# Two convolution products begun on three quarters of their columns, four tiles normalized inside attention, the last tile stored in halves

## The chip, the cores and the metric

The kernel runs on one core of a Trainium2 chip. A core has TensorE (PE, matrix products into PSUM), VectorE (DVE), ScalarE (ACT) and GpSimd (POOL), each with its own in-order queue of instructions, and SyncE (SP), whose queue here only issues DMAs; ACT's and POOL's queues issue DMAs as well. The metric is device microseconds of one execution, the median over several runs. The trace comes from one further, profiled execution.

## The reference

One sequence of T = 2048 rows of D = 1024 in float32 goes through three residual steps:

```
x = x + 0.5 * ffn(layernorm(x))
x = x + attn(layernorm(x))
x = x + 0.5 * ffn(layernorm(x))      # the same weights as the first

ffn(x):  routing = softmax(x @ gate_w.T)                 # 8 experts
         out = ((x * (routing @ in_scale)) @ sign(weight).T) * (routing @ out_scale) + bias
attn(x): q, k, v = split(conv1d(x, conv_w, width 3) + conv_b)   # 3 x 256 channels
         q, k, v -> 16 heads of 64 (wq, wk, wv and biases)
         causal softmax attention in blocks of 128 rows
         out = (heads @ wo + bo) @ proj_w + proj_b
```

## The kernel before

**Tiles and stages.** A tile is 128 rows; there are NT = 16. The first FFN goes through the tiles and, two tiles behind, normalizes its own results (`norm_x2`) and transposes them into windows for the convolution (`transpose_x2`). Then come the convolution, attention in 4 groups of 4 tiles with 8 head pairs each (32 steps), and the second FFN, which is the same class `Ffn` on other rows.

**The convolution** has width 3 and is computed with 8 transformed products per 6 rows of output, in place of 18. The transformed inputs are V[0] to V[7], each of NQ = 342 columns for each of the 8 chunks of channels; the transformed weights are the taps themselves for k = 0 and 7 (`gs`, loaded by `load_g`) and sums of them for k = 1 to 6 (`us`, made by `taps_begin` and `taps_end`). Three tiles make a window; windows 0 to 4 give 64 columns each and window 5, which has tile 15 alone, gives 22. V[0] and V[7] of a window are made by `end_transform` (three DVE instructions) as soon as the window is whole: windows 0 to 3 have their V[0] long before tile 15 is done, window 4 after tile 14, window 5 after tile 15. `store_window` makes V[7] and writes the window to DRAM; `load_window` reads it back (tile `xl`) for V[1] to V[4] (`transform`, in `conv_ends`) and once more for V[5] and V[6] (`last_transforms`), which take the memory of V[0] and V[7]. `transform` writes column a with L462, L463 and L467, column b with L466, and reads the window with L462 to L465.

**Products.** `product` takes a PSUM bank, runs 8 matmuls over the chunks (the trace shows 16 instructions, two for each float32 matmul) and has ACT copy the result out. `conv_ends` runs all six channel blocks (WORDER) with k = 0, then all six with k = 7; after that every block does k = 1 to 6 in pairs. The end of a k = 0 product frees the slot (six in `cwp`) into which SP loads the block's third tap.

**Order.** The framework places each engine's instructions at build: it simulates the program with its own estimates and takes, at each step, the earliest traced instruction that is ready. `pin` (`keep_in_program_order`) puts an instruction behind the one that was traced just ahead of it on its engine. At run time each engine goes through its fixed order.

**The second FFN's start.** `fill` returns the parts of the second FFN that run while attention drains; from step i = 32 on, one part is taken after the second and one after the fourth stage of a step. `stage_proj` of the last group is called at i = 36, ahead of the part of that place. `run` then goes through the tiles: gate of t + 2, scale of t + 1, the first half of `main`, the transposes of t + 3, the statistics of t + 4 (`norm`), the second half. `normalize` is two `bn_stats` (L155) and three small operations on DVE and POOL, and one ACT pass into `xn`. `add_bias` adds the bias to the row by a DMA on POOL's queue. A row takes one of 8 slots (`rring`): `load_rows2` fetches it, `store` writes it out.

Of the kernel before, what the change touches and what calls it, by code (L numbers as in the profile page):

```python
# [24 lines left out]
def kernel(  # L25
# [146 lines left out]
    class Ffn:  # L172
# [3 lines left out]

        def __init__(self, name, sw, work, xnp, first, end, row, ahead, after, between, beside):
            self.name, self.sw, self.work, self.xnp, self.first, self.end = name, sw, work, xnp, first, end  # L180
            self.row, self.ahead, self.after, self.between, self.beside = row, ahead, after, between, beside
            self.xns, self.xnTs, self.lgps, self.routs, self.rTs, self.oscs, self.ys = ({} for _ in range(7))
# [95 lines left out]
        def main(self, t, *halves, between=None, at=DC - 2):  # L278
            y, osc, xrow = self.ys[t], self.oscs[t], self.row(t)
            pms = {h: bank("mm", [P, NB], f"pm_{self.name}_{t}_{h}") for h in halves}  # L280
            for c in range(DC):
                if between and c == at:
                    between()
                for h, pm in pms.items():
                    for n in range(2):
                        nc.tensor.matmul(  # L286
                            pm,
                            lhsT=y[:, n, c, :],
                            rhs=self.sw[:, c, ts(h, NB)],
                            start=(c == 0 and n == 0),  # L290
                            stop=(c == DC - 1 and n == 1),
                        )
            for h, pm in pms.items():
                o, xt = osc[:, ts(h, NB)], xrow[:, ts(h, NB)]
                nc.vector.tensor_tensor(pm, pm, o, ALU.mult)  # L295
                nc.vector.tensor_tensor(xt, xt, pm, ALU.add)  # L296
            if NH2 - 1 in pms:
                del self.ys[t], self.oscs[t]

        def fill(self):  # L300

            a = self.first
            return [
                lambda: (self.norm(a), self.add_bias(a), self.norm(a + 1, True), self.add_bias(a + 1)),
                lambda: self.on(self.transpose, a),
                lambda: self.on(self.gate, a),
                lambda: (self.on(self.route, a), self.on(self.transpose, a + 1)),
                lambda: (self.on(self.turn, a), self.on(self.gate, a + 1)),
                lambda: self.scale(a, out=True),
                lambda: (self.on(self.route, a + 1), self.norm(a + 2, True), self.add_bias(a + 2)),  # L310
                lambda: (self.on(self.transpose, a + 2), self.on(self.turn, a + 1)),
                lambda: (self.norm(a + 3, True), self.add_bias(a + 3)),
            ]

        def on(self, stage, t, *more):
# [3 lines left out]
        def run(self):  # L319

            for t in range(self.first, self.end):
                self.on(self.gate, t + 2)
                if t + 1 in self.ys:
                    self.out_scale(t + 1)
                elif t + 1 < self.end:
                    self.scale(t + 1, out=True)
                route, turn = (lambda stage=stage: self.on(stage, t + 2) for stage in (self.route, self.turn))
                begun = t not in self.ys  # L330
                if begun:
                    route()
                else:
                    self.main(t, 0, between=route, at=DC // 2)
                self.on(self.transpose, t + 3)
                self.on(self.between, t - 2)
                self.on(self.norm, t + 4, t == self.first)
                self.on(self.add_bias, t + 4)
                if begun:
                    turn()  # L340
                else:
                    self.main(t, 1, between=turn, at=DC // 2)
                self.on(self.after, t - 1)
                self.beside(t)
# [50 lines left out]
    def transpose_x2(t):  # L395
        xn = x2ns.pop(t)
        n, third = divmod(t, 3)
        xw = window(n)
        at = third * P

        head = -at % 6
        tail = (at + P) % 6
        for h in range(DC // 4):
            tr = bank("acc", [P, 4, P], f"tr2_{t}_{h}")
            for c in range(4):
                nc.tensor.transpose(tr[:, c, :], xn[:, ts(4 * h + c, P)], ident)
            rows6 = xw[:, 4 * h : 4 * h + 4, :].rearrange("p c (k q) -> p c k q", q=ROW)
            q, whole = (at + head) // 6, (P - head - tail) // 6
            copy = nc.vector.tensor_copy if (t, h) == (NT - 1, 1) else nc.scalar.copy
            copy(  # L410
                rows6[:, :, :, ds(q, whole)],
                tr[:, :, head : P - tail].rearrange("p c (q k) -> p c k q", k=6),
            )
            if head:
                copy(rows6[:, :, 6 - head : 6, q - 1], tr[:, :, 0:head])
            if tail:
                copy(rows6[:, :, 0:tail, q + whole], tr[:, :, P - tail : P])
        if third == 2 or t + 1 == NT:
            end_transform(n, 0)
        if third == 0 and n > 0:  # L420
            nc.gpsimd.tensor_copy(xws[n - 1][:, :, RIGHT : RIGHT + 1], xw[:, :, 0:1])
            if t + 1 < NT:
                store_window(n - 1)
        if t == NT - 3:
            window(TRIPLES - 1)
        if third == 2 and n + 1 < TRIPLES:
            nc.gpsimd.tensor_copy(window(n + 1)[:, :, LEFT : LEFT + 1], xw[:, :, LEFT + QT : LEFT + ROW])
# [3 lines left out]
    def columns(k, n):  # L431
        return V[k][:, :, ds(n * QT, SIZES[n])]

    def end_transform(n, k):
        d = tokens(xws[n], n)
        a, b, c, e = (d[0], d[2], d[4], d[6]) if k == 0 else (d[7], d[5], d[3], d[1])
        v = columns(k, n)
        nc.vector.tensor_tensor(v, c, b, ALU.subtract)
        nc.vector.scalar_tensor_tensor(v, v, 5.25, a, ALU.mult, ALU.add)
        nc.vector.tensor_tensor(v, v, e, ALU.subtract)  # L440

    def store_window(n):
        end_transform(n, NK - 1)
        nc.sync.dma_start(out=win_dram[n], in_=xws[n])

    def load_window(n, pl):
# [61 lines left out]

    turns = iter(range(NW * NK))

    def product(w, k, uk, mp):

        acc = bank(("mm", "acc")[next(turns) // 2 % 2], [P, NQ], f"cv_{w}_{k}")
        for c in range(DC):
            nc.tensor.matmul(acc, lhsT=uk[:, c, :], rhs=V[k][:, c, :], start=(c == 0), stop=(c == DC - 1))  # L515
        m = ms.setdefault(w, {})
        m[k] = mp.tile([P, NQ], F32, name=f"m_{w}_{k}", tag=f"m{k}", bufs=NW if k in (0, NK - 1) else 1)
        if k == 1:
            nc.scalar.activation(m[k], acc, AF.Identity, bias=conv_b_sb[:, w : w + 1], scale=SCALES[k])
        else:  # L520
            nc.scalar.mul(m[k], acc, SCALES[k])  # L521

    def conv_ends(mp, tf, up, xs):
# [7 lines left out]
        for at in range(2 * NW):  # L531
            last, i = divmod(at, NW)
            w = WORDER[i]
            product(w, last * (NK - 1), gs[w, 2 * last], mp)
            if at == 0:
                for n in (TRIPLES - 2, TRIPLES - 1):
                    store_window(n)
            if not last:
                load_g(w, 2)
                if w == begun:  # L540
                    taps_begin(w, PAIRS[0], up)
                    taps_begin(w, PAIRS[1], up)
            elif i == 0:
                load_g(w, 1)
            elif i < 4:
                load_g(WORDER[1], (1, 2, 0)[i - 1])
            n, *more = jobs[at // 2]
            transform(n, 1 + 2 * (at % 2), tf)
            if more and at % 2:
                load_window(*more)  # L550
# [124 lines left out]
        ffn.run()  # L675
    norm_x2(NT - 1)
    transpose_x2(NT - 2)
    transpose_x2(NT - 1)
    ring.close()
    up = pool(b1, "up", 1)  # L680
    vm = pool(b1, "vm", 1)
# [60 lines left out]

    def store(t):
        nc.sync.dma_start(out=out[ts(t, P), :], in_=rows.pop(t))

    with ExitStack() as ph:
        ow = pool(ph, "ow", 1)
# [175 lines left out]
        for i in range(len(steps) + len(stages)):  # L923
            for n, stage in enumerate(stages):
                if 0 <= i - n < len(steps):
                    stage(*steps[i - n])
                if n == 0 and i == len(steps) - 1:

                    b2.close()
                    work = pool(f2, "work2", 2, side="right")  # L930
                    ffn = Ffn("f2", sw2, work, work, 0, NT, lambda t: rows[t], load_rows2, store, lambda t: None, lambda t: None)
                    parts = ffn.fill()
                if n == 1 and ended is not None:
                    stage_proj(ended)
# [6 lines left out]
    for part in parts:  # L941
        part()
    ffn.run()
    store(NT - 1)
    f2.close()
    b3.close()

# [52 lines left out]
```

## Time and profile before

| what | value |
|---|---|
| three runs | 995.36, 997.54, 998.24 us; median 997.54 |
| profiled execution | 995.0 us, of which the trace's span is 992.9 |
| granted TensorE clock, mean | 0.987 of full |
| FFN main product L286, 1024 matmuls | 266.6 us of PE |
| convolution L515, 768 matmuls | 223.2 us of PE |
| DMA | 143.08 MB, mean 144 GB/s |
| stretch 188 to 207 us | PE busy 11.18 of 19.00 us, clock 0.90 |
| stretch 826 to 853 us | PE busy 22.40 of 27.00 us, clock 0.94 |
| stretch 853 to 973 us | PE busy 119.52 of 120.00 us, clock 1.00 |

Times in the trace count from its first instruction. "L286" is line 286 of the kernel before. An engine's wait is put down to the instruction that released it last.

### The profile page before, as it was taken

To read this page: it belongs to the slowest core of one execution; us is meant where nothing else is said; L and a number is where in the kernel's file an instruction comes from. 1 tells how busy PE (TensorE), PEld (TensorE's weight loads), DVE (VectorE), ACT (ScalarE), POOL (GpSimd) and SP (SyncE) were. 2 spreads that over 40 slices of the span, in tenths; PEclk is the share of its full clock that TensorE was granted. 3 is DMA by queue.
4 is the path that set the end of the run, shared out by engine and by line. 5 is a ranking of instruction groups with operands and counts; after the bars stand their busy time and mean duration, and the time that the engine had idled before them with its cause. 6 is when DMAs were issued, how large, how long until landed. Compare 5 with 4: busy or idle time off the path is not lost.

```text
span 992.9 us, 13803 instructions
## 1 busy us (share of the span) xinstructions
PE 957.5 (96%) x5036; PEld 622.8 (63%) x5036; DVE 653.7 (66%) x1231; ACT 407.7 (41%) x1113; POOL 256.4 (26%) x327
## 2 busy tenths in 40 slices
PE   5999999979999999999999999999999999899997
PEld 4778888746666666655555455545554556677776
DVE  5878887798795665637656465546555656777664
ACT  4476765401011111125546244536442653545440
POOL 4455543310011111003313120212022312534321
PEclk8999999989999999999999999999999999999999
DMA  9766554698787764326030430053004217655421
GB/s 271 208 180 195 157 171 153 229 362 300 279 257 178 202 174 123 96 101 228 18 111 1 168 109 1 0 196 102 1 1 170 44 36 209 161 162 158 110 79 64
DMA packets 37252, 143.08 MB, mean 144 GB/s; under 512 B 4345, under 2 KB 5369, under 8 KB 34754
## 3 DMA queue, kind: packets, MB, share of 16 engines
q1 hardware_dynamic: 27616, 101.35, 28.0%
q0 software_dynamic: 8544, 29.64, 15.7%
q10 hardware_dynamic: 1026, 11.22, 2.9%
q8 instruction: 40, 0.66, 0.3%
q14 instruction: 26, 0.21, 0.1%
HBM read 84.37 MB, written 41.04 MB: 126 GB/s over the span
## 4 chain that ended last, share of the span: by engine, by line
PE 47%; issue 26%; DVE 11%; DMA 7%; POOL 6%; ACT 1%; SPq 0%; POOLq 0%; DVEq 0%; ACTq 0%
PE pm_f L286 18%; PE cv L515 16%; POOL xr L774 3%; PE tr_f L199 2%; PE pp L908 2%; DMA xl<-win 2%; POOL p L830 2%; PE acc L889 1%; PE lgp_f L207 1%; PE is_f L250 1%; DVE st_f L155 1%; DMA g<-in_conv_w_dram 1%; PE pq L797 1%; DMA pw_sb<-in_proj_w_dram 1%; DMA xf<-x 1%
## 5 line engine op out<-in xcount | busy, mean ns | idle before, releaser
L286 PE MATMUL pm_f<-sw,y_f 128*128 128x512 f32 x1024 | 266.6, 408 | 0.2 <-DVE x L296 0.2
L286 PEld LDWEIGHTS pm_f<-sw,y_f 128*128 128x128 f32 x1024 | 186.8, 191 | 40.9 <-DVE x L296 0.4
L515 PE MATMUL cv<-v,u 128*128 128x342 f32 x576 | 166.3, 450 | 1.1 <-DVE u L506 1.1
L515 PEld LDWEIGHTS cv<-v,u 128*128 128x128 f32 x576 | 109.0, 189 | 58.2 <-ACT m L521 1.6
L830 POOL TENSOR_SCALAR_AFFINE_SELECT p<-p 128x512 f32<-128x512 f32 x64 | 40.0, 654 | 285.9 <-ACT p L828 285.9
L843 ACT ACTIVATE p<-p,anm 128x128 f32<-128x128 f32 x256 | 99.0, 388 | 17.5 <-DVE anm L840 17.5
L264 POOL TENSOR_TENSOR y_f<-xnT_f,y_f 128x512 fp32r<-128x512 f32 x64 | 81.3, 1288 | 70.0 <-ACT y_f L263 69.2
L521 ACT ACTIVATE m<-cv 128x342 f32<-128x342 f32 x42 | 19.0, 456 | 165.8 <-PE cv L515 148.6
L828 ACT COPY p<-sc 128x512 f32<-128x512 f32 x64 | 34.3, 587 | 111.2 <-PE sc L818 111.1
L840 DVE TENSOR_REDUCE anm<-p 128x4 f32<-128x512 f32 x64 | 40.9, 681 | 49.9 <-POOL p L830 49.9
L889 PE MATMUL acc<-oT,wo_sb 128*128 128x512 f32 x128 | 66.9, 615 | 0.5 <-DVE oT L881 0.5
L515 PE MATMUL cv<-v,g 128*128 128x342 f32 x192 | 56.9, 459 | 4.7 <-DVE v L440 4.7
L295 DVE TENSOR_TENSOR pm_f<-pm_f,os_f 128x512 f32<-128x512 f32 x64 | 44.3, 692 | 25.8 <-PE pm_f L286 25.6
L797 PE MATMUL pq<-qkv,wq_sb 128*128 128x512 f32 x128 | 61.0, 596 | 0.0
L797 PE MATMUL pq<-qkv,wk_sb 128*128 128x512 f32 x128 | 60.1, 592 | 0.0
L908 PE MATMUL pp<-pw_sb,o2T 128*128 128x512 f32 x128 | 57.6, 600 | 0.5 <-DVE xr L916 0.3
L781 PE MATMUL pv<-wv_sb,qkv 128*128 128x512 f32 x128 | 56.1, 592 | 0.0
L515 PEld LDWEIGHTS cv<-v,g 128*128 128x128 f32 x192 | 37.0, 194 | 24.3 <-DVE v L440 4.9
L506 DVE SCALAR_TENSOR_TENSOR u<-g,u 128x1024 f32<-128x1024 f32 x18 | 22.0, 1223 | 40.3 <-issue 30.7
L200 ACT COPY xnT_f<-tr_f 128x512 f32<-128x512 f32 x60 | 32.5, 589 | 37.7 <-PE tr_f L199 37.7
L843 ACT ACTIVATION_READ_ACCUMULATOR p<-p,anm 128x1 f32 x256 | 47.9, 187 | 0.0
L851 DVE TENSOR_TENSOR p<-p,asum 128x512 f32<-128x512 f32 x64 | 45.6, 712 | 2.2
(143 smaller groups left out, 1482.4 us busy)
## 6 DMA issues: line engine op xcount, KB each, us to landing
g<-in_conv_w_dram SPq DMA_DIRECT2D x28, 512.0 KB, 5.3
u<-in_conv_w_dram POOLq DMA_DIRECT2D x24, 512.0 KB, 6.3
xl<-win ACTq DMA_DIRECT2D x7, 1560.0 KB, 10.9
win<-xw SPq DMA_DIRECT2D x6, 1560.0 KB, 6.0
x<-in_x_dram SPq DMA_DIRECT2D x16, 512.0 KB, 4.6
raw<-in_weight_t_dram SPq DMA_DIRECT2D x16, 512.0 KB, 6.9
x<-hbias POOLq DMA_DIRECT2D x16, 512.0 KB, 5.8
x<-x SPq DMA_DIRECT2D x16, 512.0 KB, 5.2
```

The lines of the kernel that those rows point to most:

```text
L264: nc.gpsimd.tensor_tensor(yl, y, yh.bitcast(F32), ALU.subtract)
L286: nc.tensor.matmul(pm, lhsT=y[:, n, c, :], rhs=self.sw[:, c, ts(h, NB)], start=(c == 0 and n == 0), stop=(c == DC - 1 and n == 1),)
L295: nc.vector.tensor_tensor(pm, pm, o, ALU.mult)
L515: nc.tensor.matmul(acc, lhsT=uk[:, c, :], rhs=V[k][:, c, :], start=(c == 0), stop=(c == DC - 1))
L781: nc.tensor.matmul(pv, lhsT=qkvs[g][2][:, c, ts(b, P)], rhs=wv_sb[:, c, ts(half, NB)], start=(c == 0), stop=(c == WC - 1),)
L797: nc.tensor.matmul(pq, lhsT=w_sb[:, c, ts(hp, P)], rhs=qkvs[g][n][:, c, :], start=(c == 0), stop=(c == WC - 1),)
L830: nc.gpsimd.affine_select(out=p, in_=p, pattern=[[0, BPG], [-1, P]], compare_op=ALU.is_ge, fill=NEG_INF, base=0, channel_multiplier=1,)
L840: nc.vector.tensor_reduce(nmax, p, AX.X, ALU.max, negate=True)
L843: nc.scalar.activation(p[:, b, :], p[:, b, :], AF.Exp, bias=nmax[:, b : b + 1], accum_out=asum[:, b : b + 1],)
L851: nc.vector.tensor_tensor(p, p, asum.unsqueeze(2).broadcast_to([P, BPG, P]), ALU.mult)
L889: nc.tensor.matmul(accs[g][m], lhsT=wo_sb[:, hp, ts(m, P)], rhs=oT, start=(hp == 0), stop=(hp == NHP - 1),)
L908: nc.tensor.matmul(pp, lhsT=o2T[:, m, ts(b, P)], rhs=pw_sb[:, m, ts(h, NB)], start=(m == 0), stop=(m == WC - 1),)
```

## The change

It has three parts.

1. `product_columns` computes a product on a range of columns. After `transpose_x2(NT - 2)` the first block's k = 0 product runs on its first 256 columns (FIRST = 4 x 64, windows 0 to 3), after `transpose_x2(NT - 1)` the second block's. `product` later does the remaining 86 columns of these two, and all columns of the others. Tile 15's second half is copied into its window by ACT in place of DVE. `store_window` of windows 4 and 5 pins its DVE instructions.
2. `fill` normalizes tiles 0, 1 and 2 in its first part and tile 3 in its eighth, ahead of the last group's `stage_proj` (before: tiles 0 and 1 in the first, tile 2 in the seventh, tile 3 in the ninth, behind that `stage_proj`). The second FFN takes `xn` from a pool of its own with three buffers (before: two, in `work2`), and its statistics in `run` are pinned for every tile (before: for tile 4 alone).
3. `leave` stores the last tile's halves, each behind its half of `main`; `store(NT - 1)` at the end goes away.

```diff
--- before.py
+++ after.py
@@ -176,7 +176,8 @@
 
 
 
-        def __init__(self, name, sw, work, xnp, first, end, row, ahead, after, between, beside):
+        def __init__(self, name, sw, work, xnp, first, end, row, ahead, after, between, beside, kept=1, leave=None):
+            self.kept, self.leave = kept, leave or (lambda t, h: None)
             self.name, self.sw, self.work, self.xnp, self.first, self.end = name, sw, work, xnp, first, end
             self.row, self.ahead, self.after, self.between, self.beside = row, ahead, after, between, beside
             self.xns, self.xnTs, self.lgps, self.routs, self.rTs, self.oscs, self.ys = ({} for _ in range(7))
@@ -294,6 +295,7 @@
                 o, xt = osc[:, ts(h, NB)], xrow[:, ts(h, NB)]
                 nc.vector.tensor_tensor(pm, pm, o, ALU.mult)
                 nc.vector.tensor_tensor(xt, xt, pm, ALU.add)
+                self.leave(t, h)
             if NH2 - 1 in pms:
                 del self.ys[t], self.oscs[t]
 
@@ -301,15 +303,14 @@
 
             a = self.first
             return [
-                lambda: (self.norm(a), self.add_bias(a), self.norm(a + 1, True), self.add_bias(a + 1)),
+                lambda: [(self.norm(t, t > a), self.add_bias(t)) for t in range(a, a + 3)],
                 lambda: self.on(self.transpose, a),
                 lambda: self.on(self.gate, a),
                 lambda: (self.on(self.route, a), self.on(self.transpose, a + 1)),
                 lambda: (self.on(self.turn, a), self.on(self.gate, a + 1)),
                 lambda: self.scale(a, out=True),
-                lambda: (self.on(self.route, a + 1), self.norm(a + 2, True), self.add_bias(a + 2)),
-                lambda: (self.on(self.transpose, a + 2), self.on(self.turn, a + 1)),
-                lambda: (self.norm(a + 3, True), self.add_bias(a + 3)),
+                lambda: (self.on(self.route, a + 1), self.on(self.transpose, a + 2)),
+                lambda: (self.on(self.turn, a + 1), self.norm(a + 3, True), self.add_bias(a + 3)),
             ]
 
         def on(self, stage, t, *more):
@@ -334,7 +335,7 @@
                     self.main(t, 0, between=route, at=DC // 2)
                 self.on(self.transpose, t + 3)
                 self.on(self.between, t - 2)
-                self.on(self.norm, t + 4, t == self.first)
+                self.on(self.norm, t + 4, t < self.kept)
                 self.on(self.add_bias, t + 4)
                 if begun:
                     turn()
@@ -406,7 +407,7 @@
                 nc.tensor.transpose(tr[:, c, :], xn[:, ts(4 * h + c, P)], ident)
             rows6 = xw[:, 4 * h : 4 * h + 4, :].rearrange("p c (k q) -> p c k q", q=ROW)
             q, whole = (at + head) // 6, (P - head - tail) // 6
-            copy = nc.vector.tensor_copy if (t, h) == (NT - 1, 1) else nc.scalar.copy
+            copy = nc.scalar.copy
             copy(
                 rows6[:, :, :, ds(q, whole)],
                 tr[:, :, head : P - tail].rearrange("p c (q k) -> p c k q", k=6),
@@ -431,16 +432,17 @@
     def columns(k, n):
         return V[k][:, :, ds(n * QT, SIZES[n])]
 
-    def end_transform(n, k):
+    def end_transform(n, k, pinned=False):
         d = tokens(xws[n], n)
         a, b, c, e = (d[0], d[2], d[4], d[6]) if k == 0 else (d[7], d[5], d[3], d[1])
         v = columns(k, n)
-        nc.vector.tensor_tensor(v, c, b, ALU.subtract)
-        nc.vector.scalar_tensor_tensor(v, v, 5.25, a, ALU.mult, ALU.add)
-        nc.vector.tensor_tensor(v, v, e, ALU.subtract)
-
-    def store_window(n):
-        end_transform(n, NK - 1)
+        kept = pin if pinned else lambda ins: None
+        kept(nc.vector.tensor_tensor(v, c, b, ALU.subtract))
+        kept(nc.vector.scalar_tensor_tensor(v, v, 5.25, a, ALU.mult, ALU.add))
+        kept(nc.vector.tensor_tensor(v, v, e, ALU.subtract))
+
+    def store_window(n, pinned=False):
+        end_transform(n, NK - 1, pinned)
         nc.sync.dma_start(out=win_dram[n], in_=xws[n])
 
     def load_window(n, pl):
@@ -508,11 +510,25 @@
 
     turns = iter(range(NW * NK))
 
+    accs = {}
+    FIRST = 4 * QT
+
+    def product_columns(w, k, uk, lo, hi):
+        if (w, k) not in accs:
+            accs[w, k] = bank(("mm", "acc")[next(turns) // 2 % 2], [P, NQ], f"cv_{w}_{k}")
+        for c in range(DC):
+            nc.tensor.matmul(
+                accs[w, k][:, lo:hi],
+                lhsT=uk[:, c, :],
+                rhs=V[k][:, c, lo:hi],
+                start=(c == 0),
+                stop=(c == DC - 1),
+            )
+
     def product(w, k, uk, mp):
 
-        acc = bank(("mm", "acc")[next(turns) // 2 % 2], [P, NQ], f"cv_{w}_{k}")
-        for c in range(DC):
-            nc.tensor.matmul(acc, lhsT=uk[:, c, :], rhs=V[k][:, c, :], start=(c == 0), stop=(c == DC - 1))
+        product_columns(w, k, uk, FIRST if (w, k) in accs else 0, NQ)
+        acc = accs.pop((w, k))
         m = ms.setdefault(w, {})
         m[k] = mp.tile([P, NQ], F32, name=f"m_{w}_{k}", tag=f"m{k}", bufs=NW if k in (0, NK - 1) else 1)
         if k == 1:
@@ -534,7 +550,7 @@
             product(w, last * (NK - 1), gs[w, 2 * last], mp)
             if at == 0:
                 for n in (TRIPLES - 2, TRIPLES - 1):
-                    store_window(n)
+                    store_window(n, True)
             if not last:
                 load_g(w, 2)
                 if w == begun:
@@ -675,7 +691,10 @@
         ffn.run()
     norm_x2(NT - 1)
     transpose_x2(NT - 2)
+
+    product_columns(WORDER[0], 0, gs[WORDER[0], 0], 0, FIRST)
     transpose_x2(NT - 1)
+    product_columns(WORDER[1], 0, gs[WORDER[1], 0], 0, FIRST)
     ring.close()
     up = pool(b1, "up", 1)
     vm = pool(b1, "vm", 1)
@@ -742,6 +761,11 @@
 
     def store(t):
         nc.sync.dma_start(out=out[ts(t, P), :], in_=rows.pop(t))
+
+    def leave(t, h):
+
+        if t + 1 == NT:
+            nc.sync.dma_start(out=out[ts(t, P), ts(h, NB)], in_=rows[t][:, ts(h, NB)])
 
     with ExitStack() as ph:
         ow = pool(ph, "ow", 1)
@@ -928,7 +952,7 @@
 
                     b2.close()
                     work = pool(f2, "work2", 2, side="right")
-                    ffn = Ffn("f2", sw2, work, work, 0, NT, lambda t: rows[t], load_rows2, store, lambda t: None, lambda t: None)
+                    ffn = Ffn("f2", sw2, work, pool(f2, "xn2", 3, side="right"), 0, NT, lambda t: rows[t], load_rows2, store, lambda t: None, lambda t: None, NT, leave)
                     parts = ffn.fill()
                 if n == 1 and ended is not None:
                     stage_proj(ended)
@@ -941,7 +965,6 @@
     for part in parts:
         part()
     ffn.run()
-    store(NT - 1)
     f2.close()
     b3.close()
```

## The prediction

> **What bounds the kernel now.** I read the page's busy shares first, then the waits of TensorE (PE), then stretches and order of time at the places which these waits name.
>
> ```profile
> PE 957.5 (96%) x5036; PEld 622.8 (63%) x5036; DVE 653.7 (66%) x1231; ACT 407.7 (41%) x1113; POOL 256.4 (26%) x327
> ...
> PE   5999999979999999999999999999999999899997
> ```
> PE is busy nearly throughout. So time is to be had only where PE waits or runs at a low clock; work taken from another engine brings nothing by itself.
>
> ```profile
> PE rt_f L238 <- DVE rhl_f L231: 4.7, 6, 2.3
> ...
> PE cv L515 <- DVE v L440: 4.7, 1, 4.7
> PE is_f L250 <- DVE rT_f L240: 4.0, 6, 0.9
> PE tr L406 <- DVE x2n L166: 3.2, 1, 3.2
> ...
> PE cv L515 <- DVE u L506: 1.1, 1, 1.1
> ```
> PE's waits over the span: total us, times, longest. The change touches the second and fourth (between first FFN and convolution) and, of the first and third, what lies at the start of the second FFN. The last, small here, decides below.
>
> ```profile
> 202.00:204.00 2.00, 0.36 (x4) 0.12 (x2) 2.00 (x5) 0.64 (x2) 0.00 (x0) 0.77 0.84 253
> 204.00:206.00 2.00, 0.00 (x0) 0.00 (x0) 1.99 (x5) 0.00 (x0) 1.05 (x2) 0.50 1.05 347
> 206.00:208.00 2.00, 0.97 (x2) 0.74 (x3) 2.00 (x8) 0.00 (x0) 0.00 (x0) 0.50 1.09 255
> ...
> 845.00:848.00 3.00, 0.68 (x4) 0.59 (x5) 2.47 (x5) 1.35 (x5) 3.00 (x4) 1.00 0.99 162
> 848.00:853.00 5.00, 4.16 (x34) 2.63 (x32) 2.08 (x4) 1.51 (x2) 1.63 (x4) 0.66 0.73 185
> ```
> Stretches: length, busy PE, PEld, DVE, ACT, POOL, granted PE clock, DMA share, GB/s. After each long idle time the clock is down, so an idle time costs more than its length.
>
> **Part 1, the two early products.** W0 and W1 are the first two blocks of WORDER. Before, PE ends the transposes of tile 14 at 198.1, idles 3.2, transposes tile 15 (201.3), idles 4.7 until V[0]'s last columns are there, and starts cv at 207.03. W0's 16 matmuls take 6.3 us (their end releases a DMA at 213.33), against 4.61 at full clock (ACT takes later results 4.61 apart). W1 ends at 213.3 + 4.6 = 217.9.
>
> After: 256 of 342 columns cost 256/342 x 4.61 = 3.45 us. They need windows 0 to 3 alone. That dependencies go by region, not by bounding box, this trace shows: DVE read window 4 for k=7 at 201.5 (L438), before POOL wrote that window's strided edge column at 204.1 (L421). Weights landed before 200; the PSUM banks are free at 195.0 and 198.8. So: W0's part 198.1 to 201.55; tile 15's transposes (its normalized halves end by 201.6) to 202.5; W1's part to 206.0. Meanwhile ACT makes all of tile 15's copies (before, DVE made half: 0.67 + 0.16; ACT: 0.59 + 0.17, in an ACT idle time of 11.8 us) by 203.7, and DVE window 5's end transform (3 x 0.33) by 204.9, 1.1 us in hand.
>
> The remaining 86 columns stream in 72 ns, but each of the 16 matmuls loads its weights again. The nearest row is a transpose, the same 128x128 load with a short stream: 8 in 1.03 us, 128 ns each, so 2.05 us a product. The Trainium skill (TensorE: Matmul & The Clock Gate, "The mechanism") speaks against: a weight load overlaps running matmuls only for another row group. With 128/1.2 = 107 ns, an estimate from that page's "LDWEIGHTS (loading the stationary operand)", it would be 107 + 72, 2.86 us a product. But by it a full product would take 16 x (107 + 285) = 6.3 us, and here it takes 4.61; I keep the row. Both end at 210.1, **7.8 us** sooner (6.2 by the rule).
>
> What is late next? The products' inputs follow PE until W0's last pair (k=5, 6), which waits for DVE's u L506 at 282.2 (the 1.1 us). So if DVE's chain stays, PE wins nothing there.
>
> ```profile
> 260.93 0.68 DVE L465 SCALAR_TENSOR_TENSOR vt<-xl,vt 128x512 f32<-128x512 f32 x1
> 265.15 0.69 DVE L462 SCALAR_TENSOR_TENSOR v<-xl 128x512 f32<-128x512 f32 x1 [3.54 <-DMA xl<-win]
> 265.87 0.69 DVE L463 SCALAR_TENSOR_TENSOR v<-v,xl 128x512 f32<-128x512 f32 x1
> 270.16 0.69 DVE L462 SCALAR_TENSOR_TENSOR v<-xl 128x512 f32<-128x512 f32 x1 [3.59 <-DMA xl<-win]
> 270.88 0.69 DVE L463 SCALAR_TENSOR_TENSOR v<-v,xl 128x512 f32<-128x512 f32 x1
> 271.50 0.68 DVE L466 SCALAR_TENSOR_TENSOR v<-vt,v 128x512 f32<-128x512 f32 x1
> ```
> DVE in order of time. From 207 to 261 it is full but for 3 us of waits on window loads that stay: the load that leads to them (g for W0) queues behind the window stores until 217.8 whether PE frees its slot at 213.3 or 208.1. But from 261.6 to 270.2 it does 1.4 us of work: L466 of windows 1 to 3, whose data are there, stand behind two window loads. L466 writes V[6], in V[7]'s place, free at PE's last k=7 product, 263.5 here; the scheduler, which fixes the order at build by its own estimates, put that later than the second load. ACT's order (window loads before results 10 to 12, never before 9) puts its estimate only 1 to 2 us behind the chip. With PE 6 to 8 us ahead, it should put L466 before these loads. Then DVE works on: windows 1 to 3 end at 265.2, window 0 (landed 265.1) at 268.8, window 4 (lands 270 to 271) by 274.8, window 5 by 277, u by 278.3, against 283.3. PE arrives at 282.4 - 7.8 = 274.6, waits 3.7 us, and starts about **5.2 us** earlier. The clock: the 3.2 us wait at 198 left it at 1.00, the second pulled it down and cost 6.3 - 4.6 = 1.7. For 3.7 us I take half, 0.8 (0 to 1.7). Net **4.4**. Afterwards PE was gapless to 432, so this stays. Bounds: 7.8 if DVE hides it all; -1.7 if the order stays, since then PE idles 8.9 us, starts at 283.5 as before and at a low clock.
>
> SP's other DMAs there (stores, g) keep their order and go up to 8 us sooner, into the same full queue. The pinned k=7 end transforms run one after the other, no longer between others: up to 0.7 us for DVE, covered by its 1.2 us wait at 224.9.
>
> **Part 2, normalizing earlier.** From 826 to 854 PE idles 0.8 + 0.6 + 2.3 + 0.8 = 4.6 us, and the low clock at 848 costs (3.11 - 2.11) + (1.08 - 0.65) = 1.4. The cause is DVE: tile 3's statistics stand behind the last projection (825.8), their ACT pass (828.6, 1.25) in front of the route's, and statistics of tiles 5 to 8, unpinned, run in a heap from 835 to 852, ahead of small operations that PE waits for; the last one itself waits 2.8 us for its row while rT's cast is queued behind. After: tile 2 goes with tiles 0 and 1 (rows loaded 755 to 767; the third xn buffer spares it waiting for tile 0's transposes at 792), tile 3 into tile 2's old place (811), and each later tile's statistics are pinned behind main's first half, when the row has been there for a tile's time. From 893.9 on the kernel runs 10.04 us a tile without waits; I expect nearly that from 826: of 6.0, plus 0.5 at 893, 1.5 remain. Gain **5.0** (2 to 6.5).
>
> What it adds: tile 2's 1.3 us of DVE, 0.8 of POOL, one bias DMA (0.9 on POOL) and 1.24 of ACT while attention drains. ACT's passes of tiles 0 and 1 waited for pq (their memory) until 784.06 and held up the softmax copy to 786.3; a third in that row costs up to 1.2. ACT next idles 1.1 before 789.0, so I take 0.1 within the 1.5. Tile 3's two POOL operations and bias DMA, moved ahead of the projection, meet a POOL that idles 3.0 before 813.4. SP's four row loads were already issued at 755 to 765. Queued behind a pinned statistic is rT's cast; before, it stood behind a statistic too.
>
> **Part 3, halves.** The last store leaves at 989.3 and lands 2.6 us later, 1.35 of it moving data. Half of the bytes: 0.68 less; shorter rows may cost some, so **0.6** (0 to 0.7). The first half leaves some 3.7 us earlier, beside main.
>
> **Sum**: 4.4 + 5.0 + 0.6 = 10.0. The profiled execution (995.0, of which 992.9 is span) would be 985.0. The median of the runs, 997.54, is 2.5 above it; I take the gain from the median: **987.5**.
>
> **Rivals.** (a) DVE's order stays: part 1 gives -1.7, the sum is 3.9, 993.6. For it: the stall is seen, and no view shows the new order. Against: ACT's order. (b) The second FFN's stall moves, say to rhl, which took 1.84 instead of 0.26 us beside POOL's L264: part 2 gives 1.5, 991.0. Against: these slow rhl are in the gapless stretch too. (c) Slower: the build's new estimates change the interleaving in attention, 32 steps of 8.5 us, so that acc waits for oT in each, as it did twice for 0.4 at 790 and 802. 32 x 0.4 = 12.8 against 10.0: 1000.3; it decides from 0.31 us a step. Against: attention sees the same inputs, only sooner. That a part does nothing is within the bounds.
>
> **How the numbers follow.** Forecast 0.55 (own range 984 to 991), (a) 0.25, (b) 0.12, (c) 0.08. 984 to 995.5 takes in (a) and (b) and leaves the slow end and a full gain out. 0.3% is 3 us, about what a measurement tells from no change, so faster means under 994.5: all but a little of the forecast and (b), over half of (a): 0.78. Within 0.14, slower 0.08.
>
> **What would show it.** Right: no PE wait between 197 and 210 and clock 1.00; 86-column matmuls 128 ns apart; DVE's L466 before the last two window loads; PE's wait for u 3 to 4 us; no wait over 0.5 from 826 to 854. Wrong: u's end still near 283 with PE idle 9 us before it; new PE waits per attention step; W1's part ahead of tile 15's transposes.

## The result, and the profile after

The changed kernel takes **988.58 us** (median of 6 runs, 985.7 to 992.16) against 997.64 for the kernel before (6 runs beside it): ratio 0.9911, 95% interval 0.9885 to 0.9937, so 6 to 11 us less. The forecast was 987.5. The profiled execution of the changed kernel took 990.02 us, span 988.1. Of the 13 runs of e8 below, one took 2636.84 us and is left out of its ratio.

The first rows of the page of the changed kernel (busy time and share, then TensorE's busy tenths in 40 slices):

```profile
PE 959.2 (97%) x5068; PEld 626.9 (63%) x5068; DVE 652.7 (66%) x1229; ACT 407.8 (41%) x1115; POOL 256.0 (26%) x327
...
PE   5999999999979999999999999999999999999998
```

The dents in the ninth slice, where the convolution begins, and near the end of the row, the second FFN's start, have gone. The dent in the twelfth slice (272 to 296 us) is new. PE's waits over the whole span name both:

```profile
PE cv L520 <- DVE u L508: 6.0, 2, 5.6
...
PE is_f L251 <- DVE rT_f L241: 2.6, 4, 0.9
...
PE rt_f L239 <- DVE rhl_f L232: 1.6, 4, 0.7
...
PE cv L520 <- DVE v L442: 0.8, 1, 0.8
```

The waits for V[0]'s columns fell from 4.7 to 0.8 us, the one for x2n (3.2) is gone, rhl and rT fell from 4.7 and 4.0 to 1.6 and 2.6. But the wait for u, which was 1.1 us, is now 6.0. Stretches of the changed kernel (columns as before: length, busy PE, PEld, DVE, ACT, POOL, granted clock, DMA share, GB/s):

```profile
202.00:204.00 2.00, 2.00 (x11) 1.76 (x10) 1.26 (x4) 0.98 (x2) 0.88 (x3) 1.00 1.01 374
204.00:206.00 2.00, 2.00 (x12) 1.71 (x11) 2.00 (x5) 0.00 (x0) 0.79 (x1) 1.00 0.94 260
206.00:208.00 2.00, 2.00 (x15) 1.84 (x14) 1.98 (x4) 1.22 (x4) 0.25 (x2) 1.00 0.91 324
...
281.00:283.00 2.00, 0.00 (x0) 0.00 (x0) 2.00 (x7) 0.00 (x0) 0.40 (x1) 0.50 1.05 276
283.00:285.00 2.00, 0.58 (x1) 0.50 (x2) 1.97 (x3) 0.00 (x0) 0.00 (x0) 0.50 1.04 373
285.00:287.00 2.00, 2.00 (x5) 1.18 (x4) 1.90 (x3) 0.00 (x0) 0.00 (x0) 0.50 1.04 274
287.00:289.00 2.00, 2.00 (x7) 1.26 (x6) 1.97 (x4) 0.00 (x0) 0.00 (x0) 0.81 1.03 305
845.00:848.00 3.00, 3.00 (x15) 2.41 (x14) 2.25 (x6) 0.56 (x2) 0.56 (x1) 1.00 0.46 175
848.00:853.00 5.00, 5.00 (x44) 3.79 (x44) 3.07 (x7) 3.86 (x8) 2.55 (x4) 1.00 0.42 134
```

The gap at 202 to 208 is closed at a clock of 1.00, and so is the one at 845 to 853. The loss has moved to 281: PE idle until 284.4, and then 3.3 us of work at a clock of 0.50, until 287.7 (the 0.81 is the mean of a stretch in which the clock came back to 1.00).

To say what each part brings I use stage times, since the first 197 us, which are the same code, vary by some 5 us from one profiled execution to the next. Convolution is from tile 14's first transpose to attention's first pv matmul, attention from there to the second FFN's first main matmul, the second FFN to VectorE's last instruction, the end from there to the end of the span; us, one profiled execution each. The experiments of the rows below follow.

| kernel | convolution | attention | second FFN | end |
|---|---|---|---|---|
| before | 233.92 | 395.27 | 163.06 | 3.6 |
| changed | 233.40 | 396.14 | 155.49 | 2.9 |
| e1, part 1 alone | 232.31 | 395.86 | 161.95 | 3.6 |
| e2, part 2 alone | 235.16 | 395.12 | 155.48 | 3.6 |
| e3, part 3 alone | 233.12 | 395.10 | 164.43 | 2.9 |
| e4, changed + store order | 233.32 | 393.89 | 155.74 | 2.9 |
| e5, e4 + g behind windows | 225.29 | 394.51 | 155.73 | 2.9 |
| e6, pins of part 2 alone | 233.69 | 396.60 | 157.04 | 3.6 |
| e7, fill of part 2 alone | 232.96 | 393.98 | 161.28 | 3.6 |
| e8, before + g behind windows | 233.03 | 394.99 | 164.75 | 3.6 |
| e9, changed + g behind windows | 230.52 | 394.26 | 155.74 | 2.9 |

Rows whose code is the same in a stage differ by up to 3 us, so only larger steps count. Read so, the 9 us come from the second FFN (163.55, the mean of the four rows without part 2, to 155.6) and the end (0.7); the convolution gave almost nothing.

### The profile page after: what moved, and what is told of

It reads as the page before. It is cut to its first block, busy times and chain, and to the rows that moved or that the text cites. A ratio compares the mean times of both kernels' runs of the same rounds, so it can differ in the third digit from the quotient of the medians.

```text
span 988.1 us, 13874 instructions
## 1 busy us (share of the span) xinstructions
PE 959.2 (97%) x5068; PEld 626.9 (63%) x5068; DVE 652.7 (66%) x1229; ACT 407.8 (41%) x1115; POOL 256.0 (26%) x327
## 4 chain that ended last, share of the span: by engine, by line
PE 49%; issue 31%; DVE 9%; POOL 6%; DMA 4%; ACT 1%; POOLq 0%; SPq 0%; DVEq 0%; ACTq 0%
PE pm_f L287 22%; PE cv L520 11%; POOL xr L798 3%; PE tr_f L200 3%; PE pp L932 2%; DMA xl<-win 2%; POOL p L854 2%; PE lgp_f L208 2%; PE acc L913 2%; PE is_f L251 1%; DMA win<-xw 1%; PE tr L407 1%; PE pq L821 1%; PE ao L896 1%; DVE v L469 1%
## 5 line engine op out<-in xcount | busy, mean ns | idle before, releaser
L867 ACT ACTIVATE p<-p,anm 128x128 f32<-128x128 f32 x256 | 99.0, 389 | 16.6 <-DVE anm L864 16.6
L520 PE MATMUL cv<-v,g 128*128 128x342 f32 (+2 forms) x224 | 57.1, 415 | 0.8 <-DVE v L442 0.8
L520 PEld LDWEIGHTS cv<-v,g 128*128 128x128 f32 x224 | 39.7, 190 | 17.6 <-DVE v L442 1.2
```

Of the source, the lines that this page charges most:

```text
L520: nc.tensor.matmul(accs[w, k][:, lo:hi], lhsT=uk[:, c, :], rhs=V[k][:, c, lo:hi], start=(c == 0), stop=(c == DC - 1),)
L867: nc.scalar.activation(p[:, b, :], p[:, b, :], AF.Exp, bias=nmax[:, b : b + 1], accum_out=asum[:, b : b + 1],)
```

## The experiments

**Where the convolution's gain went: what the trace says.** VectorE in order of time in the changed kernel:

```profile
224.94 0.68 DVE L466 SCALAR_TENSOR_TENSOR vt<-xl 128x512 f32<-128x512 f32 x1
233.48 0.69 DVE L464 SCALAR_TENSOR_TENSOR v<-xl 128x512 f32<-128x512 f32 x1 [7.86 <-DMA xl<-win]
...
268.13 1.29 DVE L468 SCALAR_TENSOR_TENSOR v<-vt,v 128x512 f32<-128x512 f32 x2
...
271.14 0.69 DVE L464 SCALAR_TENSOR_TENSOR v<-xl 128x512 f32<-128x512 f32 x1
...
283.05 1.22 DVE L508 SCALAR_TENSOR_TENSOR u<-g,u 128x1024 f32<-128x1024 f32 x1
```

The two late idle times of before (3.54 and 3.59 us at 265 and 270) are gone: the V[6] writes (L468 here, L466 before) now run ahead of the next windows' first reads (L464) instead of behind them. But an early wait for window 1's load is 7.86 now; before, it was 1.18, with 1.88 more for window 2:

```profile
224.92 0.69 DVE L462 SCALAR_TENSOR_TENSOR v<-xl 128x512 f32<-128x512 f32 x1 [1.18 <-DMA xl<-win]
234.10 0.69 DVE L462 SCALAR_TENSOR_TENSOR v<-xl 128x512 f32<-128x512 f32 x1 [1.88 <-DMA xl<-win]
```

The DMA issues around it on SyncE's (SPq) and ScalarE's (ACTq) queues, kernel before:

```profile
204.66 1.84 SPq L444 DMA_DIRECT2D win<-xw  x2
213.33 28.00 SPq L483 DMA_DIRECT2D g<-in_conv_w_dram  x7
213.95 0.36 ACTq L448 DMA_DIRECT2D xl<-win  x1
```

and the changed kernel, whose clock of events is 3.1 us later here:

```profile
207.77 0.87 SPq L446 DMA_DIRECT2D win<-xw  x2
211.90 29.79 SPq L485 DMA_DIRECT2D g<-in_conv_w_dram  x8
221.99 0.36 ACTq L450 DMA_DIRECT2D xl<-win  x1
```

Two things differ. The build order of SyncE's queue has the two stores swapped: window 5's goes first, and window 4's, whose buffer window 1's load takes, second. And the g loads (512 KB each) start 4.5 us earlier against the rest, because the early products free their buffers earlier. My theory was the first; the second came after e4.

**e1, e2, e3: each part alone.** The diff of each is that part of the change's diff.

> The kernel before with the convolution's part alone (early 256-column products, last copy on ScalarE, pinned end transforms). Theory: the store of window 5 now goes ahead of window 4's, so window 1's load comes 4 to 5 us late, VectorE waits about 8 us for it near 226 to 233 us, and PE still waits 5 to 6 us for u at 282 us with a clock of 0.50 after it; the part is worth 0.5 to 2 us, so about 996.5 us (0.5 to 2 below the kernel before of the same runs). Rival, the forecast's sum: 4.4 us, so 4.4 below the kernel before.

> The kernel before with the second FFN's part alone (three tiles normalized in the fill, the first NT norms pinned, three xn buffers of its own). Theory: it brings what the trace of the changed kernel shows there, 6.5 to 7 us, so 6.5 to 7 below the kernel before, with no PE wait over 0.5 us and a clock of 1.00 from the fill's end on. Rival: 5.0 as forecast, with 1.5 us of waits left at the second FFN's start. Second rival: the parts interact (attention reached earlier by the convolution's part), and alone it brings under 4.

> The kernel before with the last tile stored in two halves alone. Theory and forecast: 0.6 to 0.7 us less, all of it behind the last VectorE instruction (3.6 to 2.9 us from there to the end of the span). Rival: the second half's store, queued behind the first on SyncE's queue, lands no earlier: 0.0.

Measured, as a ratio to the kernel before with its interval: e1 0.9985 (0.9966 to 1.0005), 996.24 us; e2 0.9932 (0.9915 to 0.9948), 988.74; e3 0.9987 (0.9972 to 1.0002), 995.59. As gains from 996.51: 1.5, 6.8 and 1.3 us, together 9.6 against the changed kernel's 8.9 by its ratio: within their intervals the parts add up, and no interaction shows. The forecast's 4.4 for part 1 would be a ratio of 0.9956, outside e1's interval; in e1's trace VectorE waits 7.21 us for window 1 and PE 5.3 us for u. Part 2 is larger than forecast. e3's end is 2.9 us against 3.6, as expected; the rest of its 1.3 us is within its interval.

**e4: the store order restored.**

```diff
-        nc.sync.dma_start(out=win_dram[n], in_=xws[n])
+        (pin if pinned else id)(nc.sync.dma_start(out=win_dram[n], in_=xws[n]))
```

> The changed kernel with the two last window stores pinned, so that window 4's goes first as in the kernel before; nothing else of the order differs but one load that ScalarE issues ahead of an eviction. Theory: window 1's load lands 4 to 5 us sooner, VectorE's wait falls from 7.9 to about 3.5 us, PE's wait for u at 284 us from 5.6 to about 1.3 us, the clock stays near 1.00 there, and the time is 4 to 5.5 us below the changed kernel, about 984 us. Rival: the swap doesn't matter (the pins or the split products hold the convolution up): within 1 us of the changed kernel, 988.6 us.

Measured: 987.22 us, ratio to before 0.9912 (0.9897 to 0.9927), the changed kernel's own. **My first theory fell.** VectorE's order of time in e4:

```profile
226.44 0.69 DVE L464 SCALAR_TENSOR_TENSOR v<-xl 128x512 f32<-128x512 f32 x1 [3.73 <-DMA xl<-win]
...
236.62 0.69 DVE L464 SCALAR_TENSOR_TENSOR v<-xl 128x512 f32<-128x512 f32 x1 [2.87 <-DMA xl<-win]
```

Window 1's wait fell to 3.7 us as expected, but window 2, whose load takes window 5's place, is now late by 2.9: together 6.6 against 7.9, and PE still waits 5.7 us for u. Window 2's transfer is not slow, 10.9 us from its issue to that read; it is issued late. ScalarE's queue goes in order, and there the load stands behind a copy that waits for W0's third tap:

```profile
225.64 1.06 ACT L501 ACTIVATE u<-g 128x1024 f32<-128x1024 f32 x1 [14.34 <-DMA g<-in_conv_w_dram]
225.73 0.33 ACTq L450 DMA_DIRECT2D xl<-win  x1
```

That tap, issued at 208.99, took 16.6 us to get there; in the changed kernel, where window 1's load was not yet under way, it took 11.2. That the two loads slow each other is likely, since the DMA engines are full there, but no run shows it for this pair.

**e5: the g loads behind the windows.** The DMA engines' share from 197 to 237 us is 1.02 before, after and in e4, so I take it that no byte can be moved sooner there, only another byte instead. The groups of DMA issues in the 40 us from tile 14's first transpose on (queue, size, median us from issue to landing), before:

```profile
g<-in_conv_w_dram SPq DMA_DIRECT2D x6, 512.0 KB, 8.5
```

and changed:

```profile
g<-in_conv_w_dram SPq DMA_DIRECT2D x7, 512.0 KB, 14.1
```

The changed kernel puts seven g loads there instead of six (e4 has seven too, at 14.8 us), and the window transfers share the engines with them. e5 lets the windows go first, in ScalarE's queue, with the g loads behind them:

```diff
             if not last:
-                load_g(w, 2)
                 if w == begun:
                     taps_begin(w, PAIRS[0], up)
-                    taps_begin(w, PAIRS[1], up)
...
             if more and at % 2:
-                load_window(*more)
+                load_window(*more, True)
+                load_g(WORDER[at - 1], 2, pinned=True, queue=nc.scalar)
+                load_g(WORDER[at], 2, pinned=True, queue=nc.scalar)
+                if at == 3:
+                    taps_begin(begun, PAIRS[1], up)
```

> The kernel with the store order restored, and in it the six third-tap loads g (512 KB each) moved from SyncE's queue to ScalarE's, two at a time behind the loads of windows 1, 2 and 3; the product for u of the k=3,4 pair begins after them. Theory: the DMA engines are full from 197 to 237 us (share 1.02 to 1.04), the early products free the g buffers earlier, so the g loads start about 4 us earlier and share the engines with the window stores and loads; with the windows first, VectorE's two waits for windows 1 and 2 (3.7 and 2.9 us) fall to under 1 us together, u of the k=1,2 pair is done 4 to 6 us earlier, PE's wait for it falls from 5.7 to under 1.5 us, the clock stays at 1.00, and the time is 5 to 7 us below the kernel with the order alone (987.2): about 981. Rival: VectorE's own work or the window slots set the end of u, not the engines: VectorE's waits move to another place, PE still waits 4 us or more, 986 to 988 us.

Measured: **979.47 us**, ratio 0.9838 (0.9824 to 0.9851), better than both kernels. VectorE's order of time in e5:

```profile
221.74 0.69 DVE L464 SCALAR_TENSOR_TENSOR v<-xl 128x512 f32<-128x512 f32 x1 [0.31 <-DMA xl<-win]
...
229.91 0.69 DVE L464 SCALAR_TENSOR_TENSOR v<-xl 128x512 f32<-128x512 f32 x1 [0.85 <-DMA xl<-win]
...
272.00 1.22 DVE L508 SCALAR_TENSOR_TENSOR u<-g,u 128x1024 f32<-128x1024 f32 x1
```

and two stretches of e5, 40 and then 20 us from tile 14's first transpose on:

```profile
196.00:236.00 40.00, 39.15 (x174) 28.80 (x173) 37.75 (x75) 7.58 (x18) 4.68 (x8) 1.00 1.02 365
236.00:256.00 20.00, 20.00 (x71) 13.09 (x71) 20.00 (x31) 1.83 (x4) 0.00 (x0) 1.00 0.75 277
```

against those of the changed kernel, whose transposes begin 4.2 us later:

```profile
200.20:240.20 40.00, 39.15 (x174) 28.81 (x173) 31.06 (x64) 7.54 (x18) 4.66 (x8) 1.00 1.03 369
240.20:260.20 20.00, 19.62 (x69) 12.59 (x68) 20.00 (x33) 1.37 (x3) 0.00 (x0) 1.00 0.54 198
```

In the first both move about the same (365 and 369 GB/s), but VectorE works 37.8 of the 40 us instead of 31.1; more of the moving is done in the emptier stretch behind (share 0.75 instead of 0.54). VectorE's two waits are 1.2 us together, u starts 11.05 us earlier (4.2 of them start-up), and PE's wait for it is gone. The convolution takes 225.29 instead of 233.40 us: 5.6 of these 8.1 us are the idle time and 1.7 the low clock; 0.8 is left over, within what such stages vary by.

e5 changes two things at once, though. The `taps_begin` that it moves makes the copy which held window 2's load in e4; in ScalarE's queue the load now stands ahead of it:

```profile
218.89 0.33 ACTq L450 DMA_DIRECT2D xl<-win  x1
...
224.89 1.06 ACT L501 ACTIVATE u<-g 128x1024 f32<-128x1024 f32 x1 [5.68 <-DMA g<-in_conv_w_dram]
```

Against e4, and counted from tile 14's first transpose (197.27 there, 195.98 here), window 1's load is issued 0.6 us sooner and takes 9.0 us instead of 11.8: this is the room on the engines. Window 2's load is issued 5.5 us sooner and takes 11.0 instead of 10.9: this is its place in the queue. u starts 6.3 us sooner. A kernel with only the place in the queue changed was not run, so how the 7.4 us between e4 and e5 divide stays open.

**e8, e9: the two causes apart.** e8 is e5's g edit on the kernel before (no early products), e9 the same on the changed kernel with its own store order.

> The kernel before with the six g loads behind the window loads alone: no early products, nothing else of the change. Theory: PE itself reaches W0's pair k=5,6 only near 282 us there and waits 1.1 us for u, so room on the DMA engines can bring no more than those 1 to 2 us: 0 to 2 below the kernel before. Rival: the six moved loads bring the 7 us whatever the products do: 6 or more below the kernel before.

> The changed kernel with the six g loads behind the window loads, the two window stores left in the changed kernel's order (window 5 first). Theory: the order costs under 1 us beside the g loads, so 979 to 981 us, 7 to 9 below the changed kernel. Rival: with the engines freed, window 4's late store is the wait that remains (window 1's load issued near 222 us instead of 213), VectorE waits 3 us or more for it, and the time is 982 to 986.

Measured: e8 996.99 us, ratio 1.0003 (0.999 to 1.0015); e9 982.85, ratio 0.9853 (0.9825 to 0.9881). e8 is as expected: u starts at 278.3 us there instead of 282.1 (with a start-up 1.2 us longer), but PE, without its early products, isn't there yet. e9 falls between my theory and its rival: VectorE waits 2.93 us for window 1 and 2.73 for window 5, PE 3.4 us for u.

```profile
219.23 0.36 ACTq L450 DMA_DIRECT2D xl<-win  x1
...
225.77 0.69 DVE L464 SCALAR_TENSOR_TENSOR v<-xl 128x512 f32<-128x512 f32 x1 [2.93 <-DMA xl<-win]
```

e9 shows the engines' part alone: window 1's load is issued 21.8 us after tile 14's first transpose, as in the changed kernel, and takes 6.5 us from there instead of 11.5 (221.99 to 233.48), since the g loads now follow it in the same queue.

The store order, which alone was worth nothing (233.40 and 233.32 us in the convolution), is worth 5.2 us beside the g loads in these profiled executions (230.52 and 225.29). The whole times say 1.5 us (0.9853 less 0.9838 of 996), with intervals that overlap, so its size stays open between these. Alone it gave nothing because in e4 window 2's load, behind the copy in ScalarE's queue, lost most of what window 1's had won.

**e6, e7: the halves of part 2.** e6 keeps the old fill and only pins the statistics:

```diff
-                self.on(self.norm, t + 4, t == self.first)
+                self.on(self.norm, t + 4, t < self.kept)
```

with kept = NT for the second FFN. e7 has the new fill and the three xn buffers, with kept = 1.

> The kernel before with the second FFN's statistics pinned for all tiles, the fill and its buffers as before. Theory: what the second FFN gains comes from the normalization of tiles 2 and 3 inside attention, so the pins alone bring 0 to 1.5 us. Rival: the pins bring most of it, since they keep the statistics of tile 4 and later from slipping behind other VectorE work: 4 us or more.

> The kernel before with the new fill (three tiles normalized at once, three xn buffers of its own), the statistics after it pinned for the first tile only, as before. Theory: 5 to 7.5 us less, nearly all of what part 2 brings. Rival: without the pins the wait moves to the next tiles, and it brings under 3 us.

Measured: e6 988.82 us, ratio 0.9939 (0.9922 to 0.9956); e7 994.04, ratio 0.9982 (0.9971 to 0.9992). **My theory fell: the pins bring most of it.** In the second FFN they save 6.5 us (163.55 to 157.04), the fill 2.3; by the whole times 6.1 and 1.8. What the fill adds to the pins is 1.4 us in this stage (157.04 to 155.6), and in the whole times (e2 against e6) less than their intervals. PE's waits from 800 us on in e6:

```profile
PE rt_f L239 <- DVE rhl_f L232: 0.8, 1, 0.8
...
PE is_f L251 <- DVE rs_f L161: 0.2, 1, 0.2
```

and in e7:

```profile
PE is_f L251 <- DVE rT_f L241: 2.8, 3, 1.3
PE rt_f L239 <- DVE rhl_f L232: 1.2, 1, 1.2
PE lgp_f L208 <- ACT xnT_f L201: 0.8, 1, 0.8
```

With the fill alone, the small operations that PE waits for still stand behind the heap of statistics. The spacing of the output scales' matmuls (`po_f`, once a tile) separates the two: 11.75 and 14.97 us at first before, 11.29 and 10.08 in e6, 10.04 and 13.62 in e7. The fill removes the first loss, the pins the second.

## Why the prediction was right, and where it was not

The total was right (987.5 against 988.58), but from two errors of opposite sign: part 1 was forecast at 4.4 and is worth 0.9 (233.77, the mean of before, e2, e3, e6 and e7 in the convolution, less 232.86, that of the changed kernel and e1), part 2 was forecast at 5.0 and is worth 7.9. By the whole times of e1 and e2 they are worth 1.5 (-0.5 to 3.4) and 6.8 (5.2 to 8.5), which says the same. That the two errors cancelled is luck.

**The early products**: as forecast. W1's result leaves PE's bank at 213.75, which less the 3.1 us of start-up is 210.6 against 210.1. The clock is 1.00. The group of the 86-column matmuls in the changed kernel (count, busy us):

```profile
L520 PE MATMUL cv<-v,g 128*128 128x86 f32 x32 | 3.8, 277 | 0.8 <-DVE v L442 0.8
```

32 in 3.8 us is 119 ns each (one lasts 277 ns, so they overlap); the row of the transposes said 128. By the sentence of the Trainium skill that the forecast set against it (TensorE: Matmul & The Clock Gate, "The mechanism": weight loads overlap running matmuls only for another row group) it would have been some 179 ns, an estimate, and 5.7 us for the 32. The measurement decides against that sentence here; the same section also lets a load into a background weight buffer go ahead of running matmuls, which the forecast left out and which would fit. W1's part did begin ahead of tile 15's transposes, which I had listed as a sign against: x2n was there at 204.7, the transposes began at 205.8, and PE then waited 0.85 us for V[0]'s last columns. What that cost by itself no run shows.

**VectorE's new order**: as forecast, the late idle time is filled.

**The step that failed** is this one: "From 207 to 261 it is full but for 3 us of waits on window loads that stay: the load that leads to them (g for W0) queues behind the window stores until 217.8 whether PE frees its slot at 213.3 or 208.1." They didn't stay: 3.1 us became 7.9. g for W0 was not what led to it: the copy that waits for it began at 223.1, which is 220.0 in the time of before, 4.6 us sooner than the 224.6 there. Window 1's load came late: it was issued at 222.0, when window 4's store, now the second, had landed, which is 4.9 us later than before (214.0, or 217.1 with the start-up). Its transfer took 11.5 instead of 11.0 us, and VectorE was ready for it 1.2 us sooner; with the 1.18 us of before these make the 7.9. So the clause that failed first is "SP's other DMAs there (stores, g) keep their order". Setting the order right was not enough, since then window 2's load came late behind W0's g (e4). The second term is the g loads: I had seen the engines full (share 1.05 and 1.09 in the stretches I showed), written that SyncE's other DMAs go "up to 8 us sooner, into the same full queue", and priced that at nothing. e9 shows its price, 5.0 us of window 1's load. The swap comes with tile 15's last copy on ScalarE: in the build order of the changed kernel with that copy left on VectorE, the stores stand as before. That kernel was not run on the chip.

The rest of part 1's sum follows from it: PE arrived at u at 278.8, which is 275.7 in the time of before (forecast 274.6), and waited 5.6 instead of 3.7 us; the clock cost 1.7, the upper end I had given, instead of 0.8. So PE started at 281.3 in the time of before, 2.2 us sooner than 283.47, and less the 1.7 this leaves 0.5, as the two stages say (233.92 less 233.40). Half of 1.7 was too little for the clock in any case: after e9's wait of 3.4 us, too, PE worked 3.0 us (278.9 to 281.9) at 0.50. Rival (a), that VectorE's order stays, came nearer to part 1's size (-1.7) than the forecast did, with the wrong mechanism.

**Part 2**: mechanism right, size short. The forecast lost 6.5 us there before and let 1.5 remain. Nothing remains: from 829 us on output scales follow every 10.01 to 10.03 us, up to the last tile. And before, they stood 11.75, 14.97, 10.08, 10.14, 10.04 and 10.56 us apart, which over 10.03 is 7.4 us lost, not 6.5. I had named the heap of unpinned statistics as one cause of three; e6 shows it to be the main one.

**Part 3**: 0.7 us (3.6 to 2.9 at the end, in eleven profiles), forecast 0.6.

**Rivals (b) and (c)**: no wait replaced the second FFN's, and attention takes 393.9 to 396.6 us in all eleven, with the change or without.

## What to carry to other kernels

Where the DMA engines are full, a buffer that comes free sooner is not a gain by itself: the load that it lets go is served beside a more urgent one, which here took 11.5 us instead of 6.5. And a DMA that a compute engine's queue issues waits for what stands ahead of it there: a copy that waited for one tap held window 2's load. So before a stage is started earlier, list which transfers its end releases, whether a more urgent one is under way, and what stands ahead of that one in its queue. Putting the urgent loads first in one queue turned part 1's 0.9 us into 8.5 (233.77 to 225.29, profiled stages; by the whole times the changed kernel's 8.9 us became 16.1). Two delays of one chain may have to be removed together: the store order alone gave nothing, the g loads alone a part. And a heap of work that the scheduler may place freely, on the engine whose small operations the critical engine waits for, is worth pinning before anything is moved ahead: the pins brought 6.1 us, the earlier normalization alone 1.8.

## What the hardware showed unexpectedly

The same 512 KB load took a median of 8.5 us where six stood in the full stretch and 14.1 where seven did, while the stretch as a whole moved 362 and 369 GB/s. A wait of PE of 0.85 us at 209 left the clock at 1.00; the wait of 5.6 us was followed by 3.3 us of work at 0.50, 1.7 us lost beyond the idle time, and e9's wait of 3.4 us by 3.0 us at 0.50, nearly as much. In e4 window 2's load was issued 0.09 us after ScalarE began the copy ahead of it, which had waited 14.34 us for a transfer: a DMA in a compute engine's queue waited its turn there.
